# Attention layer and GAT layer: clamps, norm factors, first row and hand-over of the last graph layer

## The chip, the cores and the metric

One core of one Trainium2 chip runs the whole program. The metric is device time in microseconds (us), from a run of the program without profiling; the median of several runs is compared. A profile comes from one further execution.

## The reference

Eight batches of 2048 nodes with 256 features pass through two layers on one 2048 x 2048 adjacency matrix.

```python
# layer 0: attention, softmax per chunk of 256 columns
scores = clip(q @ k.T / 8, -10, 10)          # 4 heads of 64
scores = where(mask == 0, -10, scores)
out = sum over chunks of softmax(scores) @ v
out = layernorm(out @ Wo.T + bo + x) * gamma + beta
x = layernorm(x + out)
# layer 1: graph attention, softmax over all neighbours
Wh = x @ W                                    # 4 heads of 64
e[i,j] = leaky_relu(s_src[i] + s_dst[j], 0.2), -inf where adj == 0
h = elu(softmax(e, over j) @ Wh)
x = layernorm(x + h)
```

## The kernel before

All matrix work is in float32. The order of instructions on each engine is written out by hand, in the order of the Python code; each engine takes its own instructions in that order, and waits by semaphores where a tile is not ready.

**Layer 0** of one batch is 64 slots (two heads, one chunk of 256 columns, 512 rows each), taken in 32 *pairs*. In a pair, TensorE makes scores (L422, tile `ps`), VectorE clips and masks them (L439), ScalarE takes the exponential (L462), TensorE multiplies with the values (L473, tile `pc`), ScalarE copies the sums out (L480), VectorE takes reciprocals (L490) and GpSimd normalizes and adds up (L497, L499). Every eighth of these 32 pairs a new group of 512 rows begins; output products (L625) and products for layer 1 (L667) of the group before stand in some of the pairs.

**Layer 1** of the batch before runs along in the same pairs (`along`). It is 128 *tiles* in 8 *units* of 16: a unit is half of the target nodes (1024) and one head, a tile is 128 source nodes. `make` writes a tile `e` (128 x 1024, VectorE, L893): the larger of a row of the targets' factors and a factor `gd` of the source, times the edge mask. `use` multiplies it into the sums `pa` (TensorE, L922), two PSUM banks of four groups of 128 targets each. In even units each bank is a tile of its own, in odd units of the last batch both banks are one tile (`psA2`). After a unit, ScalarE copies `pa` to `sums` (L934), and `close`, a generator that `rest` takes forward by a step, clamps and inverts the weight sums (L950, L951), multiplies (L961 on ScalarE; in the last batch L955 on GpSimd), applies elu (L966, L967) and writes `h1` (L971).

A pair carries four tiles. In the last batch of layer 0 (`b == B - 1`), tiles of layer 1 of the batch before are carried while `s0 < SLOTS - LATE`; with LATE = 12 this ends with pair 25, and pairs 26 to 31 run without. The 24 tiles left over follow in a written list `order`, between the steps of the last group of layer 0 (`steps`, `early`) and the four steps of `factors` (`fs`): largest value (L734, L736, L738), spread of it (L742 to L756), and the row of the targets' factors. That last one transposes the factors (L761), copies them to `flat` (64 x 128: row h*16+t holds head h, target block t), and stores them in `rowD` in DRAM. `coming.start` then loads the row of unit 0 from there, broadcast over the partitions, into `srow`, and `lift` copies it to PSUM (`rowp`, L833). R, M, U in the list are `rest`, `make`, `use`.

**The last stage** is layer 1 of the last batch, with nothing beside it (`alone`). The row of each unit is lifted to PSUM, and VectorE makes its tiles from there. Each third tile is made by ScalarE from `srow` in SBUF (L862 Relu, L863 Identity) and by GpSimd (L864, times the mask), up to LEAD = 4 tiles ahead (`make_ahead`); these tiles have three buffers. A slot of this stage takes one or two steps of `close`, then two tiles. Beside it, `Closing` finishes the groups of 512 rows of both last batches: load `x1D`, add on GpSimd (L1009), `stats` (VectorE L540, L543, and the factors L548, L549 on VectorE, L550, L551 on GpSimd), and the scaled output on ScalarE (L588). `weigh` scales the weights of the next head on GpSimd (L770).

At the end, `last` takes the two banks of the last unit, one generator each, in turn: clamp (L1034), reciprocal, product, elu, statistics, output and store.

Of the kernel before, what the change touches and what calls it, by code (L numbers as in the profile page):

```python
# [8 lines left out]
F32 = mybir.dt.float32  # L9
# [5 lines left out]
ALU = mybir.AluOpType  # L15
AX = mybir.AxisListType

P = 128
# [4 lines left out]
def adj_resnorm_kernel(  # L23
# [19 lines left out]
    nc = tc.nc  # L43
    B, N, F = x.shape
    H, D = a_src.shape
    NT = N // P
# [3 lines left out]
    D1 = D + 1  # L50
    EPS = 1e-5
# [4 lines left out]
    QT = CH // P  # L56
    CLIP = 10.0 * 8.0
    FAR = 100.0
    BANKS = (8, 8)
# [14 lines left out]
    TILES = len(UNITS) * NT  # L74
    STEP = TILES // SLOTS
    LATE = 12
    WIDE = max(BANKS)
    AHEAD_E = 5
    LEAD = 4
# [54 lines left out]
    identf = consts.tile([P, P], F32, tag="identf", name="identf")  # L134
# [394 lines left out]
    class Norm:  # L529
# [5 lines left out]

        def stats(self, ks):
            sts = []
            for k in ks:
                st = small.tile([P, 6], F32, tag="st", name="st_" + self.name, bufs=4)
                nc.vector.bn_stats(st, self.src[:, k, :])  # L540
                sts.append(st)
            for k, st in zip(ks, sts):
                nc.vector.bn_aggr(self.mv[:, k, :], st)  # L543
            if ks[-1] == QT - 1:

                self.rs = small.tile([P, QT], F32, tag="rs", name="rs_" + self.name)
                self.off = small.tile([P, QT], F32, tag="off", name="off_" + self.name)
                nc.vector.tensor_scalar(self.rs, self.mv[:, :, 1], EPS, None, ALU.add)  # L548
                nc.vector.tensor_scalar(self.off, self.mv[:, :, 0], -1.0, None, ALU.mult)  # L549
                nc.gpsimd.tensor_tensor(self.rs, self.rs, nhalf, ALU.pow)  # L550
                nc.gpsimd.tensor_mul(self.off, self.off, self.rs)  # L551
# [169 lines left out]
    def factors(b, sd, waug):  # L721
# [8 lines left out]
        st = {}  # L730
# [27 lines left out]
        def rows():  # L758

            pr = banks([P, CH], "pr1")  # L760
            nc.tensor.transpose(pr[: H * NT, :P], s.rearrange("p h t -> p (h t)"), identf)  # L761
            flat = small.tile([H * NT, P], F32, tag="flat", name="flat", bufs=1)
            nc.scalar.copy(flat, pr[: H * NT, :P])
            nc.scalar.dma_start(out=rowD[b].rearrange("h (t p) -> (h t) p", p=P), in_=flat)
            nc.gpsimd.tensor_copy(waug[:, :, :, D], ed.rearrange("p h t -> p t h"))
            for h in range(H if b + 1 < B else 1):
                weigh(h)
# [7 lines left out]

        return gd, [most, spread, rows, weigh]


    class Layer1:
        def __init__(self, b, gd, waug):  # L780
            self.b, self.gd, self.waug = b, gd, waug
            self.made = self.used = 0
            self.rows, self.edge, self.e = {}, {}, {}
            self.tail = []
            self.room = ep, "e"
            self.alone = b == B - 1
            self.masks = {}
            self.begun, self.lifted = 0, {}
# [19 lines left out]

        def start(self):
            self.load_row(0)  # L810
            if self.alone:
                self.lift(0)
                self.ngd = small.tile([P, H, NT], F32, tag="ngd", name="ngd", bufs=1)
                nc.vector.tensor_scalar(self.ngd, self.gd, -1.0, None, ALU.mult)
# [88 lines left out]
        def use(self):  # L903
# [15 lines left out]
            e = self.e.pop(k)  # L919
            for i in range(BANKS[m]):  # L920
                for z in range(2):
                    nc.tensor.matmul(  # L922
                        self.pa[i // QT][z * D : (z + 1) * D, i % QT, :],
                        lhsT=e[:, i * P + z * D : i * P + (z + 1) * D],
                        rhs=self.waug[:, j, h, :],
                        start=(j == 0 and i % QT == 0),
                        stop=(j == NT - 1 and i % QT == QT - 1),
                        skip_group_check=True,
                    )
            self.used += 1  # L930
            if j == NT - 1 and not (self.b == B - 1 and n == len(UNITS) - 1):
                raw = small.tile([P, WIDE, D1], F32, tag="sums", name="sums", bufs=1)
                for i, pa in enumerate(self.pa):
                    nc.scalar.copy(raw[:, i * QT : (i + 1) * QT, :], pa)  # L934
                self.tail.append(self.close(n, raw))

# [4 lines left out]

        def close(self, u, raw):
            m, h = UNITS[u]
# [5 lines left out]
            dn = small.tile([P, n, 1], F32, tag="dn", name="dn")  # L949
            nc.vector.tensor_scalar(dn, raw[:, :, D:D1], 1e-30, None, ALU.max)  # L950
            nc.vector.reciprocal(dn, dn)  # L951
# [113 lines left out]
    class Closing:  # L1065
# [5 lines left out]
        def do(self, s, *kinds):  # L1071
            for g, step, *more in self.table.get(s, ()):
# [10 lines left out]
                elif step == "stats":  # L1083
                    self.of[g].n.stats((0, 1, 2, 3))
                elif step == "most":
# [87 lines left out]
    for b in range(B):  # L1173
# [169 lines left out]
        else:  # L1343
# [7 lines left out]
            order += [steps[5], U, M, M, R, U, M, U, steps[6], R, steps[7], M, M, U, steps[8], R]  # L1351
            order += [U, steps[9], M, R, M, M, U, U, R, fs[0], M, U, fs[1], M, U, fs[2], coming.start]
            done = sum(p is U for p in order) + 1, sum(p is M for p in order) + 1
# [72 lines left out]
```

## Time and profile before

| | us |
|---|---|
| median of 3 runs | 3578.28 (3577.15 to 3580.79) |
| profiled execution, its own time | 3576.82 |
| its span, first to last instruction | 3575.0 |
| pairs of the last batch until 3350 | from 2990 |
| tail of layer 0, up to the row's store | 3350 to 3394.2 |
| rest of layer 1 of batch 6 | 3394.2 to 3408.4 |
| last stage | 3408.4 to 3561.7 |
| end of the last two groups | 3561.7 to 3575.0 |

The first table of the page gives the busy share of each engine: PE 98%, DVE 85%, ACT 64%, POOL 40%. PE is TensorE, PEld its weight load, DVE VectorE, ACT ScalarE, POOL GpSimd, SP the engine that only issues transfers. A row of a timeline is: start, length (us), engine, line, operation, output<-inputs, shapes, how many were merged, and in brackets how long the engine was idle before and who ended that. A row of stretches gives the length and each engine's busy time (with instructions), then the granted clock of TensorE, the share of DMA and GB/s. A product of float32 appears as two records, so a tile's 16 products are 32 records, and a tile takes 0.93 us on PE.

### The profile page before, as it was taken

The numbers are of one execution on the slowest core, as the hardware profiler recorded it, in microseconds if no ns is written. First come the engines' busy times: TensorE is split into PE (matmuls) and PEld (weight loads), VectorE is DVE, ScalarE is ACT, GpSimd is POOL, SyncE is SP. The second block draws the span as 40 slices with busy tenths as digits, with TensorE's granted clock in tenths as the row PEclk, the third lists the DMA queues.
The fourth block names the chain that finished last, engine by engine and source line by source line (L and its number), as shares of the span: only waits on it lengthen the run. The fifth ranks groups of instructions, "written<-read, shape, count | busy, mean of one in ns | idle before, by whom it ended". The sixth has DMA issues, their size and how long they took to land. (4 is left out here: it accounts for less than half of the span.)

```text
span 3575.0 us, 170176 instructions
## 1 busy us (share of the span) xinstructions
PE 3500.7 (98%) x76892; PEld 2608.3 (73%) x76892; DVE 3041.6 (85%) x3655; ACT 2301.9 (64%) x4120; POOL 1422.8 (40%) x1255
## 2 busy tenths in 40 slices
PE   8999999999999999999999999999999999999877
PEld 5666677777777777776777767777677776777677
DVE  5886699987999689996999969999599986998798
ACT  5787556656666566665676656666576665766577
POOL 1555233333443334333343334334244342433377
PEclk9999999999999999999999999999999999999999
DMA  7653333443433444433444434433443343434332
GB/s 178 151 131 81 82 103 100 109 104 101 115 108 102 100 117 116 107 106 83 127 112 109 108 86 126 112 102 96 108 125 108 105 98 102 124 106 107 89 108 68
DMA packets 719848, 386.06 MB, mean 108 GB/s; under 512 B 433040, under 2 KB 679184, under 8 KB 719120
## 3 DMA queue, kind: packets, MB, share of 16 engines
q1 hardware_dynamic: 669120, 341.48, 37.0%
q10 hardware_dynamic: 50000, 33.70, 3.0%
q8 instruction: 601, 9.85, 1.1%
q14 instruction: 127, 1.04, 0.1%
HBM read 318.11 MB, written 56.89 MB: 105 GB/s over the span
## 5 line engine op out<-in xcount | busy, mean ns | idle before, releaser
L462 ACT ACTIVATE pr<-pr 128x1024 f32<-128x1024 f32 x960 | 996.7, 1054 | 438.0 <-DVE pr L439 364.3
L439 DVE SCALAR_TENSOR_TENSOR pr<-ps,slab 128x1024 f32<-128x1024 f32 x960 | 1115.6, 1204 | 100.3 <-PE ps L422 82.6
L893 DVE SCALAR_TENSOR_TENSOR e<-srow,gd,et 128x1024 f32<-128x1024 f32 x896 | 1165.5, 1334 | 5.2
L922 PEld LDWEIGHTS pa<-waug,e 128*64 128x64 f32 x32768 | 1002.6, 139 | 210.9 <-issue 173.3
L922 PE MATMUL pa<-waug,e 128*64 128x65 f32 x32768 | 1055.1, 223 | 32.3 <-DVE e L893 17.5
L473 PE MATMUL pc<-vaug,pr 128*64 128x65 f32 x30720 | 980.4, 222 | 6.3 <-DVE pr L439 6.0
L497 POOL TENSOR_TENSOR part<-raw,rd 128x512 f32<-128x512 f32 x446 | 473.6, 1062 | 1220.7 <-DVE rd L490 1216.6
L473 PEld LDWEIGHTS pc<-vaug,pr 128*64 128x64 f32 x30720 | 937.9, 138 | 21.8 <-DVE pr L439 18.9
L422 PE MATMUL ps<-qT,kT 64*64 64x512 f32 x8192 | 942.5, 596 | 4.9 <-DVE pr L439 2.5
L422 PEld LDWEIGHTS ps<-qT,kT 64*64 64x64 f32 x8192 | 287.3, 132 | 482.0 <-issue 269.4
L480 ACT COPY raw<-pc 128x520 f32<-128x520 f32 x512 | 302.7, 591 | 493.2 <-PE pc L473 490.3
L499 POOL TENSOR_TENSOR acc<-acc,part 128x512 f32<-128x512 f32 x446 | 583.8, 1309 | 35.1
L490 DVE RECIPROCAL rd<-raw 128x8 f32<-128x8 f32 x512 | 100.3, 196 | 129.8 <-ACT raw L480 122.6
L497 POOL TENSOR_TENSOR acc<-raw,rd 128x512 f32<-128x512 f32 x64 | 66.8, 1044 | 360.8 <-DVE rd L490 360.8
L667 PE MATMUL pw<-w_sb,x1T 128*64 128x264 f32 (+1 forms) x800 | 124.2, 392 | 0.2 <-DVE pr L439 0.2
L625 PE MATMUL po<-wo_sb,qT 128*64 128x256 f32 (+1 forms) x912 | 121.2, 382 | 0.0
L366 PE MATMUL pp<-xT,wk_sb 128*128 128x512 f32 x256 | 118.3, 602 | 2.9 <-DVE xT L322 1.6
L366 PE MATMUL pp<-xT,wq_sb 128*128 128x512 f32 x256 | 117.4, 599 | 0.0
L961 ACT ACTIVATE sums<-sums,dn 128x64 f32<-128x64 f32 x448 | 117.1, 334 | 0.0
L382 PE MATMUL pv<-wv_sb,xT 128*128 128x256 f32 x512 | 116.7, 381 | 0.0
L382 PEld LDWEIGHTS pv<-wv_sb,xT 128*128 128x128 f32 x512 | 96.0, 190 | 20.1 <-issue 7.2
L893 DVE SCALAR_TENSOR_TENSOR e<-rowp,gd,et 128x1024 f32<-128x1024 f32 x86 | 104.0, 1269 | 0.0
(142 smaller groups left out, 2517.5 us busy)
## 6 DMA issues: line engine op xcount, KB each, us to landing
et<-edgeD SPq DMA_DIRECT2D x896, 128.0 KB, 2.6
slab<-clipD SPq DMA_DIRECT2D x256, 256.0 KB, 3.7
srow<-rowD SPq DMA_DIRECT2D x256, 128.0 KB, 3.5
xg<-in_x_dram SPq DMA_DIRECT2D x128, 128.0 KB, 3.2
x1D<-y ACTq DMA_DIRECT2D x32, 512.0 KB, 2.9
ctxD<-acc ACTq DMA_DIRECT2D x56, 256.0 KB, 3.7
ctx<-ctxD SPq DMA_DIRECT2D x224, 64.0 KB, 2.9
xp<-in_x_dram SPq DMA_DIRECT2D x224, 64.0 KB, 2.2
```

The costliest lines, as they stand in the source:

```text
L366: nc.tensor.matmul(pps[c], lhsT=w[:, kc, c * P : (c + 1) * P], rhs=st["xT"][:, kc, :], start=(kc == 0), stop=(kc == KC - 1),)
L382: nc.tensor.matmul(pv[:, u, :], lhsT=st["xT"][:, kc, u * P : (u + 1) * P], rhs=wv_sb[:, kc, :], start=(kc == 0), stop=(kc == KC - 1),)
L422: nc.tensor.matmul(ps[z * D : (z + 1) * D, k, :], lhsT=kT[rows, hp, t * P + z * D : t * P + (z + 1) * D], rhs=qT[rows, hp, cols], start=Tr ...
L439: nc.vector.scalar_tensor_tensor(pr, ps, -CLIP, row.unsqueeze(1).to_broadcast([P, 2, CH]), op0=ALU.max, op1=ALU.min,)
L462: nc.scalar.activation(pr, pr, AF.Exp, scale=0.125)
L473: nc.tensor.matmul(pc[z * D : (z + 1) * D, k, to], lhsT=probs[s][u][:, k, i * P + z * D : i * P + (z + 1) * D], rhs=vaug[:, KT * c + u, 2 ...
L480: nc.scalar.copy(raws[s].rearrange("p k i d -> p k (i d)"), pc[:, :, : QT * D1])
L497: engine.tensor_mul(part, raw[:, :, :, :D], rd.to_broadcast([P, 2, QT, D]))
L499: engine.tensor_add(accv, accv, part)
L667: nc.tensor.matmul(pw[z, k, : F + 2 * H], lhsT=self.x1T[:, c, u * P + z.start : u * P + z.stop], rhs=w1_sb[:, c, :], start=(c == 0), stop= ...
L893: nc.vector.scalar_tensor_tensor(e, row, self.gd[:, h, j : j + 1], self.mask(k), op0=ALU.max, op1=ALU.mult,)
L922: nc.tensor.matmul(self.pa[i // QT][z * D : (z + 1) * D, i % QT, :], lhsT=e[:, i * P + z * D : i * P + (z + 1) * D], rhs=self.waug[:, j, h ...
```

## The change

It has five parts.

1. `LATE` goes from 12 to 8: pairs 26 and 27 carry tiles of layer 1 of batch 6 as well, and 16 tiles instead of 24 are left for the list.
2. The row of unit 0 of the last stage is made by TensorE: eight products with a broadcast column of the identity matrix put eight rows of `flat` on all partitions, straight into the PSUM tile. ScalarE's tiles of unit 0 read that tile too. The load of this row and its lift are left out.
3. `stats` of the closing groups puts the two small operations L548 and L549 on GpSimd.
4. `close` in the last stage clamps from `pa` in PSUM, one instruction per bank, and no longer from `sums`.
5. Of the last four tiles, TensorE takes the products of the first bank as each tile comes; those of the second bank follow for all four together.

```diff
-    LATE = 12
+    LATE = 8
...
-        def stats(self, ks):
+        def stats(self, ks, beside=False):
...
-                nc.vector.tensor_scalar(self.rs, self.mv[:, :, 1], EPS, None, ALU.add)
-                nc.vector.tensor_scalar(self.off, self.mv[:, :, 0], -1.0, None, ALU.mult)
+                engine = nc.gpsimd if beside else nc.vector
+                engine.tensor_scalar(self.rs, self.mv[:, :, 1], EPS, None, ALU.add)
+                engine.tensor_scalar(self.off, self.mv[:, :, 0], -1.0, None, ALU.mult)
                 nc.gpsimd.tensor_tensor(self.rs, self.rs, nhalf, ALU.pow)
                 nc.gpsimd.tensor_mul(self.off, self.off, self.rs)
...
+            st["flat"] = flat
...
+        def first_row(dst):
+
+            for t in range(WIDE):
+                nc.tensor.matmul(
+                    dst[:, t * P : (t + 1) * P],
+                    lhsT=identf[: H * NT, t : t + 1].to_broadcast([H * NT, P]),
+                    rhs=st["flat"],
+                    start=True,
+                    stop=True,
+                )
...
-        def start(self):
-            self.load_row(0)
-            if self.alone:
-                self.lift(0)
+        def start(self, first_row=None):
+            if not self.alone:
+                self.load_row(0)
+            else:
+                self.lifted[0] = psA.tile([P, WIDE * P], F32, tag="psA0", name="rowp")
+                first_row(self.lifted[0])
+                self.rows[0] = self.lifted[0]
                 self.ngd = small.tile([P, H, NT], F32, tag="ngd", name="ngd", bufs=1)
                 nc.vector.tensor_scalar(self.ngd, self.gd, -1.0, None, ALU.mult)
...
+            if self.alone and k >= TILES - LEAD:
+
+                products(e, j, range(QT))
+                self.held.append((e, j))
+                if k == TILES - 1:
+                    for each in self.held:
+                        products(*each, range(QT, BANKS[m]))
+            else:
+                products(e, j, range(BANKS[m]))
...
-            nc.vector.tensor_scalar(dn, raw[:, :, D:D1], 1e-30, None, ALU.max)
+            if self.alone:
+                for i, pa in enumerate(pas):
+                    k = slice(i * QT, (i + 1) * QT)
+                    nc.vector.tensor_scalar(dn[:, k, :], pa[:, :, D:D1], 1e-30, None, ALU.max)
+            else:
+                nc.vector.tensor_scalar(dn, raw[:, :, D:D1], 1e-30, None, ALU.max)
...
-                    self.of[g].n.stats((0, 1, 2, 3))
+                    self.of[g].n.stats((0, 1, 2, 3), True)
...
-            order += [U, steps[9], M, R, M, M, U, U, R, fs[0], M, U, fs[1], M, U, fs[2], coming.start]
+            order += [U, steps[9], M, R, M, M, U, U, R, fs[0], M, U, fs[1], M, U, fs[2], lambda: coming.start(fs[4])]
```

More of the change, by code (lines that the diff above doesn't have):

```diff
@@ L774, in weigh @@
             )
-        return gd, [most, spread, rows, weigh]
+        def first_row(dst):
[7 more added lines that the diff above has]
+                )
+        return gd, [most, spread, rows, weigh, first_row]
     class Layer1:
@@ L783, in __init__ @@
             self.rows, self.edge, self.e = {}, {}, {}
-            self.tail = []
+            self.tail, self.held = [], []
             self.room = ep, "e"
@@ L919, in use, with products @@
             e = self.e.pop(k)
[L920 to L929, printed above, removed]
+            def products(e, j, tiles):
+                for i in tiles:
+                    for z in range(2):
+                        nc.tensor.matmul(
+                            self.pa[i // QT][z * D : (z + 1) * D, i % QT, :],
+                            lhsT=e[:, i * P + z * D : i * P + (z + 1) * D],
+                            rhs=self.waug[:, j, h, :],
+                            start=(j == 0 and i % QT == 0),
+                            stop=(j == NT - 1 and i % QT == QT - 1),
+                            skip_group_check=True,
+                        )
+            if self.alone and k >= TILES - LEAD:
[6 more added lines that the diff above has]
+                products(e, j, range(BANKS[m]))
             self.used += 1
@@ L934, in use @@
                     nc.scalar.copy(raw[:, i * QT : (i + 1) * QT, :], pa)
-                self.tail.append(self.close(n, raw))
+                self.tail.append(self.close(n, raw, self.pa))
         def rest(self, steps):
@@ L940, in rest, with close @@
                     self.tail.pop(0)
-        def close(self, u, raw):
+        def close(self, u, raw, pas):
             m, h = UNITS[u]
```

## The prediction

> **What bounds the kernel.** I read the page first: TensorE is busy for 98% of the span, yet its busy digits fall from 9 to 7 and 8 in the last slices. So I cut the end into stretches by engine. The last stage runs from 3408.4 to 3561.7 us; its units end where the sums are copied (L934). Columns: length, then busy time of PE, PEld, DVE, ACT, POOL.
>
> ```profile
> 3296.46:3307.10 10.64, 9.43 (x181) 6.00 (x177) 6.58 (x8) 8.81 (x16) 4.06 (x4) 1.00 0.40 97
> 3212.69:3225.63 12.94, 12.94 (x306) 9.65 (x305) 10.76 (x13) 5.86 (x9) 5.87 (x6) 1.00 0.23 64
> ...
> 3430.40:3453.90 23.50, 17.85 (x534) 17.18 (x530) 23.40 (x34) 18.14 (x24) 21.06 (x14) 0.93 0.30 90
> 3473.70:3491.60 17.90, 15.88 (x534) 15.60 (x530) 14.99 (x15) 17.61 (x23) 12.69 (x9) 1.00 0.38 120
> sum 153.50, PE 128.27 PEld 124.99 DVE 138.63 ACT 127.65 POOL 122.84; mean PE 16.03 PEld 15.62 DVE 17.33 ACT 15.96 POOL 15.35
> ```
>
> Pairs that carry tiles of layer 1 are full on PE (12.94 of 12.94); those without are not. In the last stage no engine stands out: DVE has 138.6 of 153.5 us, ACT 127.7, POOL 122.8. The second unit (3430.4) is DVE's, with POOL close behind; the fourth is ACT's.
>
> Next, DVE's timeline there, and POOL's beside it:
>
> ```profile
> 3432.56 1.79 DVE L548 TENSOR_SCALAR rs_c<-mv_c 128x4 f32<-128x4 f32 x1
> 3434.27 2.05 DVE L549 TENSOR_SCALAR off_c<-mv_c 128x4 f32<-128x4 f32 x1
> 3436.24 2.05 DVE L950 TENSOR_SCALAR dn<-sums 128x8 f32<-128x8 f32 x1
> ...
> 3434.28 3.97 POOL L864 TENSOR_TENSOR e<-e,et 128x1024 f32<-128x1024 f32 x2
> 3439.46 1.93 POOL L770 TENSOR_TENSOR waug<-waug,ed 128x1024 f32<-128x1024 f32 x1
> ```
>
> Operations on 4 or 8 elements take 1.8 to 2.05 us: they end when a POOL product ends (2.0 us). With POOL idle the same lines take 0.16. Last, the hand-over from layer 1 of batch 6 to that of batch 7:
>
> ```profile
> 3394.25 0.46 ACTq L764 DMA_DIRECT2D rowD<-flat  x1
> 3402.38 1.02 ACT L833 COPY rowp<-srow 128x1024 f32<-128x1024 f32 x1 [8.16 <-DMA srow<-rowD]
> 3407.63 0.84 ACT L934 COPY sums<-pa 128x260 f32<-128x260 f32 x2 [4.23 <-PE pa L922]
> 3408.37 1.15 ACT L862 ACTIVATE e<-srow,ngd 128x1024 f32<-128x1024 f32 x1
> ```
>
> ACT and POOL stand idle for 12 us while DVE alone makes the eight tiles left over.
>
> **The parts.**
>
> *LATE 12 to 8.* Pairs 26 and 27 now carry four tiles each. Both have an output product, as 3212.69 has: 12.94 − 10.63 = 2.31 us each, **+4.6**. PE is full there, so nothing else in them counts. In the tail, 16 tiles are left; the 14 makes and uses written between the steps stay, and eight makes after the factors (3395.55 to 3406.77) are gone, with eight of the ten uses. Unit 6 of batch 6 now ends in pair 27, so its closing moves one place up in the written order. That frees ACT of L934 before the group's finish (3379.68: the transposes come 1.2 us earlier), but its last step, L971 on DVE, now stands ahead of the maximum (L734) and waits for ACT's Relu: estimate 3390.7 instead of 3389.87. L736 needed PE anyway until 3390.93, so up to the flat row (ACT ends it at 3394.22) I count **0**.
>
> *First row.* Removed: four row DMAs on SP, the lift on ACT. The write of rowD stays, for the next rows. PE waits for the flat row, then does 8 products, 16 records. Nearest row: L382, 256 columns at 0.216 us a record; 128 columns give 0.108, so 1.7 us (0.213 each, as cold transposes took, would give 3.4). Then two uses, 2 × 0.93, and 0.3 until ACT's first Relu, as before (3408.05 to 3408.37): 3394.3 + 1.7 + 1.9 + 0.3 = 3398.2 against 3408.37, **−10.2**.
>
> PE's wait for the flat row (ACT, 3393.98 to 3394.22) holds back only these two uses; on SP the next row's load now is the first to wait for rowD's landing (some 3397), and behind it stand x1D loads that POOL's add needs four slots later: no cost.
>
> That holds only if DVE and ACT can both read the row. ACT's Relu used srow in SBUF; for unit 0 it now reads the PSUM tile that DVE reads. The row that bears on this: the mask tile, which DVE reads and then ACT.
>
> ```profile
> 40.50 0.81 DVE L272 TENSOR_SCALAR clip<-pm 128x640 int8<-128x640 bf16 x1
> ...
> 41.34 0.69 ACT L274 CAST edge<-pm 128x640 fp8e4<-128x640 bf16 x1 [0.56 <-DVE clip L272]
> ```
>
> In all 48 such pairs ACT started after DVE's end. The Trainium skill (PSUM — Partial Sum Buffer, "PSUM bank collisions raise a hardware error") says why software must order even two reads: two engines in one bank at once is an error. Free reads give −10.2. Ordered reads chain Relu and products in program order: Relu(2), e0, Relu(5), e1, clamp and reciprocal, e3, Relu(8), e4, e6, Relu(11), e7, e9; with 1.15 per Relu, 1.2 to 1.25 per tile, 0.05 per hand-over, then ACT's Identity, exp, Relu (1.25) and lift, Relu(14) begins 14.8 us after Relu(2), against 12.9 before (3408.37 to 3421.31). So 1.9 is lost: **−8.3**. I take this. Behind the new wait stand all of DVE's tiles and, with them, PE: the first starts at 3399.5, after Relu(2), which itself stands behind the copies L934, and not at 3396.1, when the row is there.
>
> *Factors on POOL.* L548 and L549, six each in the stage, held DVE for 10.7 us. POOL gets 12 operations of a kind the trace lacks. Nearest row: L551, 4 elements, 0.20 (L550, a power, 1.0, and the strided copy L765, 1.0, are the upper end). Against the change speaks the skill's GPSIMD Engine Reference, "Elementwise — side-by-side cycle accounting": GpSimd takes 1.96 times DVE's time, 0.31 here by DVE's 0.16. By the row, unit 1's two groups cost POOL 0.8, by the rule 1.25. I take the row. The new pair waits for DVE's aggregates, as the power did before, so nothing behind it on POOL waits longer than these 0.4 us a group.
>
> *Clamps from PSUM.* Seven of L950 took 7.5; now 14 like L1034 (0.16), 2.2. L1034 ran with POOL idle, but DVE's tiles from the PSUM row take 1.27 whether POOL is busy or not, whereas those from srow reach 2.9. Stretched like L950 (1.07 mean) they would cost 15. I take 0.16. They still come behind L934 by the ordering above.
>
> DVE is thus 10.7 + 5.3 = 16.0 us lighter. **What reaches the end** I read unit by unit. Unit 1: DVE's stall of some 7 us (3432.6 to 3438.3, and L548 at 3442.5) goes, and PE's gaps of 2.2 and 1.6 us with it; late next is POOL, busy without a pause from 3423.8 to 3449.7. Its tile 26 was ready at 3444.35, tile 29 at 3447.7; with the added operations 3444.8 and 3448.5. PE then ends the unit at 3451.3 instead of 3453.8; a slower clock after the new gap could cost 1. I take **−2.0**. Unit 2: PE waits for POOL and for its own issue (2.5 at 3462.59), 0. Unit 3: ACT, 17.6 of 17.9, 0. Unit 4: PE nearly full, 0. Unit 5 and the start of 6: the chain goes through POOL's h (L1009) and e, then ACT, busy until 3545, **0**. Unit 7:
>
> ```profile
> 3544.34 0.70 ACT sums L934 x2
> 3545.06 1.56 DVE dn L950
> 3546.64 0.20 DVE dn L951
> 3546.85 1.16 DVE e L893
> ...
> 3549.24 12.38 PE pa L922 x416
> 3561.72 0.17 DVE dn L1034
> ```
>
> The clamp shrinks from 1.56 to 0.32: **−1.2**, PE being nearly full from there.
>
> *Bank by bank.* The first bank would be done 1.9 instead of 0.5 us before PE's end. But unit 7's two banks are one tile, and before, the first clamp (3561.72) already waited for the very last product, although its bank was finished at 3561.1; unit 1's copies did too. So **0**; were it tracked by bank, −1.2. The held tiles block no buffer, as none is made after them; tile 127 now must be ready 2.3 us before PE's end, which it is (3559.3, less 1.2).
>
> **Sum**: 4.6 − 8.3 − 2.0 − 1.2 = −6.9. The profiled execution took 3576.8 around a span of 3575.0, so 3569.9; the median of the runs is 1.5 above it: 3578.3 − 6.9 = **3571.4 us**.
>
> **Rivals.** (B) DVE was the bound of the whole stage, and its relief passes on. For it: 138.6 of 153.5, the highest. Against: units 3, 5, 6. With half of the 16 us reaching the end instead of 3.2, the sum is −11.7: 3566.6. Free reads (−1.9) or banks tracked singly (−1.2) point the same way. (C) POOL takes back what DVE gives: unit 1 gains 0, the end 0: 4.6 − 8.3 = −3.7, 3574.6. For it: POOL's unbroken stretch. (D) Slower: POOL's new scalar operations cost like L550. At p each, if all 12 lie on POOL's chain, the sum is −6.9 + 12 (p − 0.2); it turns at p = 0.78, and at 1.4 us gives +7.5: 3585.8. Against: L551, and that units 3, 4 and 7 have slack on POOL. (E) The moved tiles merely exchange places: unlikely, since 2.31 a pair is measured, and 12 us of idle ACT are too.
>
> **Numbers.** Main case 0.42, its own range 3568.5 to 3574; B 0.32; C 0.14; D and unknown stalls 0.12. Range: below 3564.5 lies a part of B, above 3578.5 most of D, together 0.2. 0.2%, about what a measurement of this kernel can tell from no change, is 7.2 us, just beyond the main case's sum. Faster: half of the main case and B, 0.53; same: the other half, C and a little of D, 0.36; slower 0.11.
>
> **What would show it.** Periods of 12.9 in pairs 26 and 27; L862 first near 3398 + 4.6, with no lift ahead of it; in unit 0 Relu and DVE's tiles never overlapping; small POOL operations near 0.2; no L548 over 0.2 us in the stage; a second unit near 21 us, POOL full; the first L1034 still behind PE's last product. It would be wrong if POOL's new rows are long, if PE's slow clock spreads over unit 0, where it is now fed more thinly, or if the freed DVE lets units 2 to 6 shrink.

## The result and the profile after

The changed kernel takes 3572.81 us (median of 22 runs, 3569.59 to 3578.09), the kernel before, on the same chip, 3579.23 us (22 runs, 3577.15 to 3583.48). The ratio is 0.9983, 95% interval 0.9977 to 0.9990: a gain of 6.4 us. A repeat beside other kernels gave 0.9989 (0.9982 to 0.9995). The prediction had 3571.4 us, with a range of 3564.5 to 3578.5, and the time lies in it; the gain stays just under the 0.2% that the prediction set as its mark, the case that it called "same" and gave 0.36, against 0.53 for "faster". The profiled execution took 3571.87 us around a span of 3570.0.

The stretches of the changed kernel come first, in the columns of the stretches of before. Line numbers have moved: L548, L549 are now L549, L550; L588 is L589; L862 to L864 are L878 to L880; L893 is L909; L922 is L940; L934 is L962; L950 is L981; L971 is L1004; L1009 is L1042; L1034 is L1067.

```profile
3298.62:3311.60 12.98, 12.98 (x308) 9.95 (x304) 12.38 (x13) 8.94 (x16) 4.65 (x4) 1.00 0.41 113
...
3426.39:3452.21 25.82, 17.77 (x536) 17.22 (x532) 18.27 (x32) 18.14 (x24) 23.15 (x19) 0.93 0.30 91
...
3470.91:3488.84 17.93, 16.07 (x536) 15.65 (x532) 15.01 (x16) 17.65 (x24) 14.86 (x13) 1.00 0.36 118
...
sum 152.52, PE 128.12 PEld 125.36 DVE 125.41 ACT 127.63 POOL 125.04; mean PE 16.01 PEld 15.67 DVE 15.68 ACT 15.95 POOL 15.63
```

Pair 26 is full on PE, as forecast, and the fourth unit is ScalarE's and unchanged. DVE is lighter by 13.2 us over the stage (138.6 to 125.4), and yet the second unit, where this was to help, grew from 23.50 to 25.82 us. POOL is busy for 23.15 of them.

The hand-over to the last stage, from the timelines of TensorE, ScalarE and VectorE:

```profile
3399.65 2.05 PE L781 MATMUL rowp<-flat,identf 64*128 64x128 f32 x16 [0.36 <-ACT flat L765]
...
3403.30 0.84 ACT L962 COPY sums<-pa 128x260 f32<-128x260 f32 x2 [3.70 <-PE pa L940]
3404.03 1.12 ACT L878 ACTIVATE e<-rowp,ngd 128x1024 f32<-128x1024 f32 x1
...
3405.19 1.28 DVE L909 SCALAR_TENSOR_TENSOR e<-rowp,gd,et 128x1024 f32<-128x1024 f32 x1 [4.78 <-ACT e L878]
3407.66 1.28 DVE L909 SCALAR_TENSOR_TENSOR e<-rowp,gd,et 128x1024 f32<-128x1024 f32 x1 [1.18 <-ACT e L878]
```

The row's products took 2.05 us from the first start to the last end, and the first Relu starts 4.43 us behind the end of the copy to `flat`, instead of 14.15. VectorE's first tile waits for the end of ScalarE's Relu, and its second for the end of the next: two reads of one PSUM tile, one after the other. The groups of the last stage show the other small operations (busy time, mean in ns, idle time before them):

```profile
L909 DVE SCALAR_TENSOR_TENSOR e<-rowp,gd,et 128x1024 f32<-128x1024 f32 x86 | 104.2, 1270 | 8.8 <-ACT e L878 8.8
...
L981 DVE TENSOR_SCALAR dn<-pa 128x4 f32<-128x4 f32 x14 | 1.6, 152 | 6.0 <-ACT sums L962 5.9
L549 POOL TENSOR_SCALAR rs_c<-mv_c 128x4 f32<-128x4 f32 x6 | 1.4, 234 | 0.5
L550 POOL TENSOR_SCALAR off_c<-mv_c 128x4 f32<-128x4 f32 x6 | 1.4, 228 | 0.5
```

Clamps from PSUM take 0.15 us with POOL busy beside them; the factors take 0.23 each on GpSimd. VectorE waits 8.8 us for ScalarE's reads of the first row. And the second unit, from the timelines of GpSimd, ScalarE, VectorE and TensorE:

```profile
3420.93 2.02 POOL L880 TENSOR_TENSOR e<-e,et 128x1024 f32<-128x1024 f32 x1 [2.24 <-issue]
...
3442.26 0.23 POOL L549 TENSOR_SCALAR rs_c<-mv_c 128x4 f32<-128x4 f32 x1
...
3443.89 0.20 POOL L552 TENSOR_TENSOR off_c<-off_c,rs_c 128x4 f32<-128x4 f32 x1
3444.04 3.98 POOL L880 TENSOR_TENSOR e<-e,et 128x1024 f32<-128x1024 f32 x2
...
3444.12 2.08 ACT L589 ACTIVATE kT<-h,off_c,rs_c 128x256 f32<-128x256 f32 x4 [0.36 <-POOL off_c L552]
...
3446.23 2.34 DVE L1004 SCALAR_TENSOR_TENSOR h<-ee,sums 128x512 f32<-128x512 f32 x1 [7.52 <-ACT kT L589]
...
3449.82 7.82 PE L940 MATMUL pa<-waug,e 128*64 128x65 f32 x250 [2.14 <-DVE e L909]
```

Read it upwards: TensorE waits for VectorE's tile, which stands behind the write of `h` of unit 0 (L1004). This write waits 7.52 us for ScalarE's output of the second closing group (L589), which must have read these rows of the tile `h` before they are written again. The write itself then takes 2.34 us and ends 0.55 us behind GpSimd's two products beside it (3448.57 against 3448.02). ScalarE's output waits for GpSimd's factors of the group, and they stand in a queue that is busy without a pause from 3420.93 to 3448.02.

Last, the end, from the chain of work that ended last:

```profile
3540.38 0.64 ACT sums L962 x2
3541.05 0.17 DVE dn L981
3541.24 0.20 DVE dn L984
3541.45 6.35 DVE e L909 x6
...
3549.15 4.78 DVE e L909 x4
3553.98 2.58 PE pa L940 x80
3556.65 0.17 DVE dn L1067
```

The clamp of 1.56 us is now 0.17. Behind VectorE's last tile (3553.93) TensorE still has 80 records: 16 of the last tile's first bank and the 64 held ones. The last clamps begin behind the very last product.

### The profile page after: what moved, and what is told of

Its sections match the earlier page's. It is cut to its first block, busy times and chain, and to the rows that moved or that the text cites. A ratio compares the mean times of both kernels' runs of the same rounds, so it can differ in the third digit from the quotient of the medians.

```text
span 3570.0 us, 170208 instructions
## 1 busy us (share of the span) xinstructions
PE 3500.0 (98%) x76908; PEld 2606.1 (73%) x76908; DVE 3026.1 (85%) x3650; ACT 2302.1 (64%) x4119; POOL 1426.6 (40%) x1267
## 5 line engine op out<-in xcount | busy, mean ns | idle before, releaser
L909 DVE SCALAR_TENSOR_TENSOR e<-srow,gd,et 128x1024 f32<-128x1024 f32 x896 | 1165.3, 1334 | 5.1
L940 PEld LDWEIGHTS pa<-waug,e 128*64 128x64 f32 x32768 | 1001.2, 138 | 206.9 <-issue 173.1
L940 PE MATMUL pa<-waug,e 128*64 128x65 f32 x32768 | 1053.1, 223 | 27.9 <-POOL e L880 15.5
L382 PE MATMUL pv<-wv_sb,xT 128*128 128x256 f32 x512 | 116.6, 381 | 0.0
L909 DVE SCALAR_TENSOR_TENSOR e<-rowp,gd,et 128x1024 f32<-128x1024 f32 x86 | 104.2, 1270 | 8.8 <-ACT e L878 8.8
L382 PEld LDWEIGHTS pv<-wv_sb,xT 128*128 128x128 f32 x512 | 95.9, 190 | 20.3 <-issue 6.9
```

Of the source, the lines that this page charges most:

```text
L382: nc.tensor.matmul(pv[:, u, :], lhsT=st["xT"][:, kc, u * P : (u + 1) * P], rhs=wv_sb[:, kc, :], start=(kc == 0), stop=(kc == KC - 1),)
L909: nc.vector.scalar_tensor_tensor(e, row, self.gd[:, h, j : j + 1], self.mask(k), op0=ALU.max, op1=ALU.mult,)
L940: nc.tensor.matmul(self.pa[i // QT][z * D : (z + 1) * D, i % QT, :], lhsT=e[:, i * P + z * D : i * P + (z + 1) * D], rhs=self.waug[:, j, h ...
```

## The experiments

Each kernel computes the whole result. "Flat" is the end of ScalarE's copy to `flat`; a unit's length runs between ScalarE's copies of the sums (L962), unit 7's to TensorE's last product. Times are in us, from one trace each. The ratio is to the kernel before in the same set of runs, with the 95% interval.

| kernel | first Relu behind flat | unit 0 ends behind flat | unit 1 | unit 2 | unit 7 | median | ratio |
|---|---|---|---|---|---|---|---|
| before | 14.15 | 36.17 | 23.50 | 19.79 | 17.26 | 3579.23 | |
| changed | 4.43 | 26.79 | 25.82 | 18.70 | 16.15 | 3572.81 | 0.9983 (0.9977-0.9990) |
| e_again | 4.44 | 26.79 | 27.07 | 18.69 | 16.15 | 3576.09 | 0.9989 (0.9982-0.9995) |
| e_before_late8 | 8.82 | 31.28 | 23.08 | 19.49 | 17.26 | 3579.20 | 0.9996 (0.9987-1.0004) |
| e_late12 | 14.15 | 36.50 | 25.82 | 18.71 | 16.15 | 3580.45 | 1.0002 (0.9994-1.0010) |
| e_own_copy | 4.44 | 25.34 | 26.49 | 20.25 | 16.15 | 3576.28 | 0.9989 (0.9980-0.9997) |
| e_dve_factors | 4.43 | 26.78 | 25.82 | 18.26 | 16.15 | 3575.24 | 0.9987 (0.9980-0.9993) |
| e_clamp_sums | 4.43 | 26.78 | 25.84 | 18.71 | 17.59 | 3579.72 | 0.9997 (0.9989-1.0006) |
| e_no_bank | 4.44 | 26.79 | 25.81 | 18.69 | 15.81 | 3576.32 | 0.9986 (0.9978-0.9994) |
| e_early_closing | 4.44 | 26.79 | 22.04 | 18.69 | 16.15 | 3571.56 | 0.9974 (0.9964-0.9984) |
| e_before_early | 14.15 | 35.60 | 21.89 | 18.26 | 17.26 | 3576.96 | 0.9992 (0.9984-1.0000) |
| e_early_dve | 4.43 | 26.79 | 21.29 | 18.25 | 16.15 | 3567.35 | 0.9968 (0.9957-0.9979) |
| e_own_early | 4.43 | 25.31 | 23.85 | 18.72 | 16.15 | 3570.42 | 0.9973 (0.9964-0.9982) |
| e_own_early_dve | 4.43 | 25.31 | 21.21 | 18.25 | 16.14 | 3569.06 | 0.9969 (0.9957-0.9981) |

Medians are compared through the ratios: the kernel before had 3579.90 beside e_own_copy, e_dve_factors, e_clamp_sums and e_no_bank, 3579.83 beside e_again, e_early_closing, e_own_early and e_before_late8, 3580.00 beside e_before_early, e_early_dve and e_late12, and 3580.34 beside e_own_early_dve.

### The changed kernel again

> The changed kernel once more, beside the others of this job. Theory: pairs 26 and 27 12.9 us each, first Relu 4.4 us behind the flat row, unit 1 at 25.8 us. The stretch from pair 30 to the flat row (55.1 us in the profile of the changed kernel, 56.4 to 56.7 in three of its variants) and unit 4 (14.5) should vary by 1 to 1.6 us between executions if they belong to TensorE's clock and not to an edit; the rival, that they belong to the kernel, expects 55.1 and 14.5 again.

No edit. Where no clock is in play, the structure repeats to 0.02 us: the first Relu, units 2, 3 and 7, and TensorE's last wait in unit 1, which ends 50.22 us behind flat in the one trace and 50.20 in the other. Other parts do not repeat: pair 30 to flat took 55.07 us in the first trace and 56.73 here, unit 1 25.82 and 27.07 (at granted clocks of 0.93 and 0.81), unit 5 19.34 and 20.93. Unit 5 in the stretches of the first trace:

```profile
3503.30:3522.64 19.34, 15.83 (x536) 15.55 (x532) 18.93 (x33) 16.22 (x17) 17.48 (x13) 1.00 0.18 58
```

and of the repeat:

```profile
3506.68:3527.61 20.93, 17.42 (x535) 17.14 (x531) 18.97 (x32) 16.23 (x17) 18.70 (x13) 0.92 0.18 54
```

The same products keep PE busy for 1.59 us more at a granted clock of 0.92, and the unit is longer by just that. The Trainium skill (TensorE: Matmul & The Clock Gate, "What's actually happening") says that the clock follows a free-running window, so that it depends on the run where a ramp falls; these two traces agree in that the same code met it in one execution and not in the other. Tail, unit 1 and unit 5 together are 4.5 us in this pair of traces (1.66 + 1.25 + 1.59), so one trace of each kernel can't carry a sum of 5 us, and units are compared below with their clocks. Unit 4 took 14.46 and 14.83, at a clock of 1.00 in both, a smaller difference than the 1 to 1.6 us expected of the clock; it ranges from 14.44 to 16.86 over the variants of the changed kernel and from 15.81 to 16.05 over the three of the kernel before. The longer ones go with a wait of TensorE late in the unit, up to 1.2 us, that the profile gives to its own issue; what moves it stays open.

### LATE alone, and all but LATE

> The kernel before with four tiles in pairs 26 and 27 and no other edit: the first row still comes through the row DMAs and ACT's lift. Theory: pairs 26 and 27 at 12.9 us, +4.6; the first Relu falls from 14.15 to about 10.3 us behind the flat row, since the DMA that was hidden behind eight tiles is now waited for (the lift began 8.2 us behind the flat row's DMA issue), -3.9; sum +0.7, so about 3580, and of the 9.7 us that the row gains in the changed kernel some 6 need TensorE's row. Rival: the row DMA is hidden anyway, the first Relu comes at 4.4 to 6 us, and the time falls by 3 us or more.

```diff
 # in the kernel before
-    LATE = 12
+    LATE = 8
```

ScalarE's timeline of e_before_late8:

```profile
3398.91 0.24 ACT L763 COPY flat<-pr 64x128 f32<-64x128 f32 x1
...
3406.49 1.02 ACT L833 COPY rowp<-srow 128x1024 f32<-128x1024 f32 x1 [7.33 <-DMA srow<-rowD]
3407.44 0.65 ACT L934 COPY sums<-pa 128x260 f32<-128x260 f32 x2
3407.97 1.16 ACT L862 ACTIVATE e<-srow,ngd 128x1024 f32<-128x1024 f32 x1
```

The transfer that eight tiles had hidden is now waited for: lift, copies and Relu follow each other without a gap. The first Relu gains 5.3 us (14.15 to 8.82; 3.9 was expected), the pairs cost 4.6 (12.94 each), and the time is 0.9996: about nothing, as the theory said. TensorE's row is needed for the other 4.4 us (8.82 to 4.43).

> The changed kernel with twelve slots without tiles, as before the change, and everything else kept. Theory: pairs 26 and 27 fall to 10.6 us each, -4.6; the eight tiles stand again between the factors and unit 1, and the start of ACT's Relu is set by DVE's eight makes behind the factors and no longer by the row: about 10 us later. Sum +5 against the changed kernel, near 3579, and TensorE's row is worth nothing there. Rival: the eight tiles need not come first, and unit 0's end moves by less than 3 us: the time falls by 2 us against the changed kernel.

```diff
 # in the changed kernel
-    LATE = 8
+    LATE = 12
```

ScalarE's and VectorE's timelines of e_late12:

```profile
3395.36 0.24 ACT L765 COPY flat<-pr 64x128 f32<-64x128 f32 x1
...
3409.01 0.84 ACT L962 COPY sums<-pa 128x260 f32<-128x260 f32 x2 [13.41 <-PE pa L940]
...
3396.93 11.29 DVE L909 SCALAR_TENSOR_TENSOR e<-srow,gd,et 128x1024 f32<-128x1024 f32 x8
```

The eight tiles stand in front again, and the first Relu is back at 14.15, to the hundredth that of the kernel before, though the row is there early. The ratio is 1.0002. So neither LATE alone nor the four other parts without it gain, and together they gain: LATE opens a hole that only TensorE's row fills.

### The first row copied for ScalarE

> The changed kernel, but ScalarE copies the first row from PSUM into SBUF as soon as TensorE has made it (1.0 us, while ScalarE would wait for TensorE anyway), and makes its tiles of unit 0 from that copy. Theory A, ordered reads of one PSUM tile cost 1.6 us: VectorE's first tile starts 2.4 us earlier, Relu of tile 14 comes 13.0 instead of 14.5 us after that of tile 2, and the kernel gains 1.5 us on the changed one. Rival: the ordering is hidden behind GpSimd's queue in the second unit: less than 0.5 us.

```diff
 # in the changed kernel
-                self.rows[0] = self.lifted[0]
+                self.rows[0] = small.tile([P, WIDE * P], F32, tag="srow", name="srow")
+                nc.scalar.copy(self.rows[0], self.lifted[0])
```

VectorE's, then TensorE's timeline of e_own_copy (the added line moves later line numbers by one):

```profile
3404.70 2.48 DVE L910 SCALAR_TENSOR_TENSOR e<-rowp,gd,et 128x1024 f32<-128x1024 f32 x2 [2.37 <-ACT srow L829]
...
3407.41 4.81 DVE L910 SCALAR_TENSOR_TENSOR e<-rowp,gd,et 128x1024 f32<-128x1024 f32 x4
...
3450.22 9.40 PE L941 MATMUL pa<-waug,e 128*64 128x65 f32 x250 [2.56 <-DVE e L910]
```

With ScalarE reading its own copy, VectorE makes four tiles in one go, and the fifth Relu starts 12.94 us behind the first instead of 14.49: the cost of the ordered reads is 1.55 us, shown by taking it away. Unit 0 ends 1.45 us earlier, and GpSimd's queue passes this on: TensorE's last wait in unit 1 ends 48.71 us behind flat (3450.22 - 3401.51), instead of 50.22. What is lost after that, this trace loses at a lower clock. The last 70 records of unit 1 then take 3.1 us instead of 2.4, and unit 2 ran at 0.87 in this trace, where the changed kernel had 1.00, and took 20.25 instead of 18.70. The ratio, 0.9989, can't show 1.5 us with an interval of some 3 us to either side, so whether the clock takes it in most executions stays open.

### The factors back on VectorE

> The changed kernel with the factors of the closing groups made on VectorE again. Theory A (the last stage is paced by hand-overs between GpSimd, ScalarE and TensorE; VectorE's time matters at few places): -1 to +2.5 us against the changed kernel, although VectorE gets some 10 us of stalled operations back; the second unit stays at 24 to 26 us because its write of h1 still waits for the second closing group's output. Theory B (VectorE was the bound, and its relief passes on): +5 us or more, the second and sixth unit each longer by some 3 us.

```diff
 # in the changed kernel
-                    self.of[g].n.stats((0, 1, 2, 3), True)
+                    self.of[g].n.stats((0, 1, 2, 3))
```

Unit 1 stays at 25.82 us. VectorE is stretched again (its L549, L550 take 1.80 and 2.04 us there), its write of `h` waits 1.69 instead of 7.52, and the tile that TensorE waits for comes 1.3 us sooner behind flat (48.9 against 50.2). This doesn't arrive, since the products behind that wait ran at half the clock. The stretch of e_dve_factors from TensorE's wait to the end of unit 1:

```profile
3449.30:3453.01 3.71, 3.69 (x72) 3.69 (x74) 3.54 (x3) 0.00 (x0) 0.87 (x1) 0.54 0.81 241
```

In the changed kernel the corresponding 72 records took 2.35 us at a clock of 1.00. Unit 2 is 0.44 shorter, at a clock of 1.00 in both, and this holds through the table: at that clock unit 2 takes 18.25 to 18.26 us in the four kernels with the factors on VectorE and 18.69 to 18.72 in the seven with them on GpSimd. Unit 5, at a clock of 0.92, takes 20.48 where the repeat took 20.93, since TensorE waits 2.29 instead of 2.74 us for GpSimd's tile. The ratio, 0.9987, lies between the two of the changed kernel: theory A's bounds hold, and moving the factors to GpSimd brought nothing that can be measured.

### The clamps back on the copied sums

> The changed kernel with the clamps reading sums in SBUF again. Theory A: +1.2 us against the changed kernel, all of it in the last unit (16.2 becomes 17.3 us), where the clamp of the unit before stands ahead of the tiles; elsewhere stalls of 1.5 to 2 us come back on VectorE without effect. Theory B: +3 to +5 us.

```diff
 # in the changed kernel
-            if self.alone:
-                for i, pa in enumerate(pas):
-                    k = slice(i * QT, (i + 1) * QT)
-                    nc.vector.tensor_scalar(dn[:, k, :], pa[:, :, D:D1], 1e-30, None, ALU.max)
-            else:
-                nc.vector.tensor_scalar(dn, raw[:, :, D:D1], 1e-30, None, ALU.max)
+            nc.vector.tensor_scalar(dn, raw[:, :, D:D1], 1e-30, None, ALU.max)
```

VectorE's timeline of e_clamp_sums at the start of the last unit:

```profile
3548.23 1.60 DVE L978 TENSOR_SCALAR dn<-sums 128x8 f32<-128x8 f32 x1 [4.12 <-ACT sums L962]
```

One clamp of 1.60 us, on the chain of unit 7, lengthens this unit by 1.44 (16.15 to 17.59); unit 1 does not notice (25.84). Over the stage, eight clamps take 7.2 us where fourteen from PSUM take 1.6. The Trainium skill (SBUF — State Buffer, "SBUF: two separate sides") describes a port pair of VectorE and GpSimd that one holds for a whole instruction; the clamps agree with it: in SBUF they took 0.90 us in the mean and up to 1.93, from PSUM 0.15 and at most 0.16. The time rose more than unit 7 explains: 0.9997 against 0.9983 and 0.9989, and 3.4 to 4.5 us over the medians of the three other variants in the same set of runs, which is what theory B had expected. Units 4 and 5 of its trace are longer too (16.86, 20.93). For unit 5 the repeat above shows the same length without the edit; in unit 4 TensorE has two waits on its own issue (0.75 and 1.18 us), which nothing ties to the clamps. So 1.44 us are shown to be the clamp's, and whether the other 2 to 3 us are stays open.

### The last tiles in one piece

> The changed kernel without the bank-by-bank order of the last four tiles. Theory A (a wait on a PSUM tile covers the whole tile): within 0.5 us of the changed kernel, the first clamp of the end still right behind TensorE's last product. Rival (banks are waited for singly): +1.2 us.

```diff
 # in the changed kernel
-            if self.alone and k >= TILES - LEAD:
+            if False:
```

VectorE's timeline of e_no_bank:

```profile
3551.13 4.86 DVE L909 SCALAR_TENSOR_TENSOR e<-rowp,gd,et 128x1024 f32<-128x1024 f32 x4
3558.38 0.16 DVE L1067 TENSOR_SCALAR dn<-pa 128x4 f32<-128x4 f32 x1 [2.39 <-PE pa L940]
```

The last clamp waits for the last product here too, 2.39 us behind VectorE's last tile instead of 2.73 in the changed kernel, and unit 7 is 0.34 shorter. Bank by bank therefore gains nothing at the end, since both banks are one tile, and costs 0.3: VectorE's last tile sets the end, and more products are left behind it. In the medians this doesn't show: the ratio, 0.9986, lies between the two of the changed kernel.

### The closing groups two steps earlier

> The closing groups of batch 6 begin two steps earlier. Theory: unit 1 is late because DVE's write of h for unit 0 (7.5 us of waiting) stands behind ACT's output of the second closing group, which stands behind GpSimd's factors of that group. With the group two steps earlier the wait falls by 2 to 4 us and unit 1 from 25.8 to 22 to 24 us; the time is 2 to 3 us below the changed kernel. Rival: GpSimd's total work paces unit 1 and the order in it is of no account: unit 1 stays within 0.5 us of 25.8, and the time within 1 us.

```diff
 # in the changed kernel
-        0: [(0, "load", kT, 0)],
-        2: [(1, "load", kT, 1)],
-        4: [(0, "pool")],
-        6: [(1, "pool")],
-        8: [(0, "stats")],
-        9: [(2, "load", kT, 2)],
-        10: [(1, "stats")],
-        11: [(0, "finish")],
+        0: [(0, "load", kT, 0), (1, "load", kT, 1)],
+        2: [(0, "pool")],
+        4: [(1, "pool")],
+        6: [(0, "stats")],
+        8: [(1, "stats")],
+        9: [(2, "load", kT, 2), (0, "finish")],
+        11: [(1, "finish")],
         12: [(3, "load", kT, 3)],
-        13: [(1, "finish")],
```

VectorE's and TensorE's timelines of e_early_closing:

```profile
3443.56 2.52 DVE L1004 SCALAR_TENSOR_TENSOR h<-ee,sums 128x512 f32<-128x512 f32 x1 [3.56 <-ACT sums L1000]
...
3434.89 7.39 PE L940 MATMUL pa<-waug,e 128*64 128x65 f32 x192 [2.31 <-POOL e L880]
3443.62 7.29 PE L940 MATMUL pa<-waug,e 128*64 128x65 f32 x234 [1.33 <-POOL e L880]
```

The write of `h` no longer waits for L589 but for its own input, and for half as long. Unit 1 falls by 3.8 us to 22.04, at the same clock (0.92, 0.93 in the first trace of the changed kernel), and beside the repeat of the changed kernel the median falls by 4.5 us, from 3576.09 to 3571.56; 2 to 3 were expected. GpSimd does the same work, but both its adds L1042 lie in unit 0, where the changed kernel's queue had a pause of 2.24 us. So the order counts, and not the total of GpSimd's work alone. The edit takes the wait away and one add of 2.4 us out of unit 1 at once; no run moves only the write behind VectorE's next tiles, which would part the two.

> The kernel before with the closing groups of batch 6 two steps earlier and no other edit. Theory: before, DVE was stopped in unit 1 by its own stretched factor and clamp operations and not by ACT's output (its write of h waited for nothing), so the earlier group gains little there: unit 1 stays at 22.5 to 24 us (23.5 before), and the time within 1.5 us of the kernel before. Rival: the order of the closing is a gain by itself that has nothing to do with the change: unit 1 falls by 3 us or more here too, and the time by 3 us.

The same edit in the kernel before. Unit 0 ends 0.6 us earlier and unit 1 falls by 1.6 to 21.89, at clocks of 0.92 and 0.93. (Unit 2 is 1.5 shorter, but ran at 1.00 here and at 0.91 in the trace of before.) The ratio is 0.9992 (0.9984 to 1.0000). So the earlier order is worth something by itself: in unit 1 more than the theory's bound and less than the rival's 3 us, in the medians the rival's 3 us (3580.00 to 3576.96). The theory had overlooked that the factors move too: in unit 1 two of VectorE's small operations are stretched (1.80 and 1.99 us), where there were four. With the change the order is worth 3.8 us in unit 1.

> The changed kernel with the earlier closing and the factors back on DVE. Theory: with the wait for ACT's output gone, the relief of DVE that was worth nothing in unit 1 is worth something: with the factors on DVE unit 1 lasts 23 to 24.5 us instead of 22.0 (two to four operations stretched to 2 us, less GpSimd's 0.9), the time 1 to 3 us above the earlier closing alone. Rival: GpSimd's chain alone sets unit 1, which stays at 22.0 +- 0.5 or falls by the 0.9 us that GpSimd no longer spends.

```diff
 # in e_early_closing
-                    self.of[g].n.stats((0, 1, 2, 3), True)
+                    self.of[g].n.stats((0, 1, 2, 3))
```

VectorE's, then TensorE's timeline of e_early_dve:

```profile
3424.18 1.66 DVE L549 TENSOR_SCALAR rs_c<-mv_c 128x4 f32<-128x4 f32 x1
3425.76 1.96 DVE L550 TENSOR_SCALAR off_c<-mv_c 128x4 f32<-128x4 f32 x1
...
3441.05 0.82 DVE L1004 SCALAR_TENSOR_TENSOR h<-ee,sums 128x512 f32<-128x512 f32 x1 [0.42 <-ACT sums L1000]
...
3428.95 18.25 PE L940 MATMUL pa<-waug,e 128*64 128x65 f32 x564 [4.10 <-DVE e L909]
```

I had expected unit 1 to be 1 to 2.5 us longer; it is 0.75 shorter (21.29), and unit 2 0.44 shorter. VectorE has its two stretched operations again (3.6 us), TensorE waits 4.10 us for its tile at the start of the unit, and then runs to the end without one more wait: GpSimd is no longer in front of it. The clock is 0.92 in unit 1 of both kernels. By the trace the rival was right: with the order mended, GpSimd's amount of work counts. With 3567.35 us, 0.9968 (0.9957 to 0.9979), this kernel has the lowest median of all; the changed kernel had 0.9983 and 0.9989 in two other sets of runs. Against e_early_closing alone (0.9974, 0.9964 to 0.9984) the intervals overlap, so the time doesn't show the factors' part.

### The row's copy on top

> The earlier closing together with ACT's copy of the first row in SBUF. Theory: the copy alone started e0's follower 2.4 us earlier and lost this in units 1 and 2, since the write of h stands behind the closing group; with that group earlier too, the 1.5 us of unit 0 remain, and the time is 1 to 2 us below the earlier closing alone, about 3568. Rival: GpSimd's queue is full whatever the order, the 1.5 us are lost again, and the time is that of the earlier closing alone.

The edits of e_own_copy and e_early_closing together. Unit 0 gains 1.48, but unit 1 is 1.8 longer (23.85 against 22.04). The stretch from TensorE's last wait in unit 1 to its end, of e_own_early:

```profile
3443.20:3450.71 7.51, 7.44 (x200) 7.45 (x202) 7.30 (x5) 4.36 (x5) 6.14 (x4) 0.77 0.76 232
```

and of e_early_closing:

```profile
3443.60:3449.73 6.13, 6.09 (x200) 5.95 (x202) 6.13 (x5) 4.31 (x5) 5.71 (x3) 1.00 0.60 174
```

The last wait ends 41.72 us behind flat instead of 42.72, so GpSimd passes on 1.0 of the 1.48; the same 200 records then take 1.35 us more, at 0.77 instead of 1.00. The medians of the two, from one set of runs, are 1.1 us apart in favour of the copy, the ratios 0.0001. Neither theory is settled by the time; by the trace, GpSimd's queue keeps a third of the gain, and the clock took the rest in this execution.

> The earlier closing, the factors on DVE and ACT's copy of the first row together. Theory: GpSimd's queue sets the end of unit 1 as long as it is unbroken; with the factors on DVE it had 2.3 us of waiting inside unit 1, so the copy's gain in unit 0 (1.5 us, 26.8 to 25.3) now passes through and unit 1 stays within 0.6 us of the 21.3 that it had with the earlier closing and the factors on DVE: 1 to 1.5 us below that kernel, ratio to the kernel before near 0.9964. Rival: as with the factors on GpSimd, unit 1 gives back 1.5 to 1.8 us (22.8 to 23.1) and the time does not move.

The same with the factors on VectorE. Unit 0 has the 1.48 us, and unit 1 keeps its length (21.21 against 21.29) as the theory said, though with the better clock of the two (1.00, 0.92), so that the trace alone doesn't prove it. The medians (3569.06 of 6 runs, 3567.35 of 7 runs of e_early_dve; ratios 0.9969 and 0.9968, each with an interval of 0.11 to 0.12% to either side) can't show 1.5 us, so its worth in time stays open.

## Why the prediction came out as it did

The steps of the sum, with the profiled pair beside them (before against after, us), and the repeat where it differs. The ordered reads are taken up to the start of GpSimd's unbroken stretch (29.54 us behind flat before, 21.33 after), and unit 1 from there to its end:

| step | predicted | measured | repeat |
|---|---|---|---|
| pairs 26 and 27 | +4.6 | +4.65 | +4.95 |
| tail up to flat | 0 | -1.43 | +0.23 |
| first Relu behind flat | -10.2 | -9.72 | |
| ordered reads | +1.9 | +1.51 | |
| unit 1, beyond the row | -2.0 | +1.15 | +2.4 |
| unit 2 | 0 | -1.09 | |
| units 3 and 6 | 0 | -0.01 | |
| unit 4 | 0 | -1.59 | -1.22 |
| unit 5 | 0 | +0.41 | +2.00 |
| unit 7 | -1.2 | -1.11 | |
| end behind the last product | 0 | +0.04 | |
| ahead of pair 26 (same code) | | +2.16 | +1.96 |

The column of the first pair adds up to -5.03, the difference of the spans. At like clocks unit 2 is not shorter but 0.44 longer (18.26 us in e_before_early, 18.70 in the changed kernel), and the edits account for 4.65 - 9.72 + 1.51 + 1.15 + 0.44 + 0.41 - 1.11 = -2.7. Unit 4 gives some -0.9 more, if the mean of the table's kernels is taken for both sides (16.0 for three of the kernel before, 15.1 for ten of the changed one without e_clamp_sums). The medians say -6.4 and -3.7. The traces of before and after are one draw each; the start of pair 26 shows it, at 3296.5 in the trace of before and at 3296.7 to 3300.1 in the others, with the same code ahead of it in all. The tail is another such draw: 75.05 to 76.72 us over the eleven kernels with LATE 8, 76.49 in the trace of before.

**Pairs.** Right: PE is full in a pair with tiles, and 12.94 could be read off a neighbour.

**First row.** Right in mechanism and size. The products' records start 0.112 us apart, where 0.108 was taken from L382; with a first step of 0.21 and the last record's own 0.27 they took 2.05 us, not 1.7, and the Relu came 4.43 us behind flat where 4.0 was counted. The choice between free and ordered reads was right as well: 1.51 of the predicted 1.9, and the copy takes it away. The skill's reason (PSUM — Partial Sum Buffer, "PSUM bank collisions raise a hardware error") fits, but no run tests what would happen without the order.

**Unit 1.** This is the step that failed: "DVE's stall of some 7 us goes, and PE's gaps of 2.2 and 1.6 us with it; late next is POOL". The stall did go, and POOL did become late, by what had been counted: its unbroken stretch grew from 25.94 us (3423.76 to 3449.70) to 27.09 (3420.93 to 3448.02). Each operation took 0.23 us, nearer to the row of 0.20 than to the 0.31 estimated from the ratio in the skill's GPSIMD Engine Reference ("Elementwise — side-by-side cycle accounting"), which was measured with 2048 elements; yet the four cost 1.15 with the gaps between them, nearer to the 1.25 of that estimate than to the row's 0.8. But the unit did not end behind POOL's last tile, which was ready at 3446.03, 6 us ahead of the end. The write of `h` stands in VectorE's order ahead of the tiles that end the unit, and it needs the closing group's output, which needs POOL. In the kernel before, from the timelines of ScalarE, VectorE and GpSimd:

```profile
3446.38 2.06 ACT L588 ACTIVATE kT<-h,off_c,rs_c 128x256 f32<-128x256 f32 x4
...
3449.14 1.10 DVE L971 SCALAR_TENSOR_TENSOR h<-ee,sums 128x512 f32<-128x512 f32 x1
...
3445.70 4.00 POOL L864 TENSOR_TENSOR e<-e,et 128x1024 f32<-128x1024 f32 x2
```

Before, VectorE reached this write 25.4 us behind the start of POOL's stretch because it was stalled itself, 0.7 us after ScalarE's output was done (3448.44): of its 7 us of stall no more than these 0.7 could have been saved here. Now it writes at 25.3 us, because it waits there: 7 us of stall became 7.52 us of waiting. The write also ends about 0.5 us behind POOL's products in both kernels (3450.24 and 3449.70 before, 3448.57 and 3448.02 after; the same in e_dve_factors, e_early_closing and e_early_dve), so a later POOL stretches it, from 1.10 to 2.34 us, and from its end to the end of the unit there are 3.6 us in both. From the start of POOL's stretch, unit 1 thus ends after 31.28 us instead of 30.13: all of POOL's 1.15 came through, by way of the stretched write, and nothing of VectorE's relief did. (The unit's own length grew by 2.3, since unit 0, which POOL does not end, gained 1.17 more than the start of POOL's stretch.) I had looked at what VectorE's freed time would let TensorE do, and not at the next wait in VectorE's own queue. e_early_closing takes that wait away and gets 3.8 us in this unit; by the trace of e_early_dve the factors are better on VectorE even then, by 1.2 us in units 1 and 2.

**Unit 7 and the banks.** Right to 0.1 us for the unit; e_clamp_sums shows that it is the clamp. That the last clamp waits for the whole tile was right. "tile 127 now must be ready 2.3 us before PE's end, which it is" missed the point: PE ends 2.6 us behind that tile, held by it, and the held products cost 0.3 us instead of nothing.

**Units 2, 4 and 5.** All three were counted as 0. Unit 2 shrank by 1.1 in the pair of traces: the trace of before had a clock of 0.91 there (so had e_before_late8, with 19.49), that of the changed kernel 1.00, and at like clocks it grew by 0.44. Unit 5 grew by 0.4 at a clock of 1.00 in both. e_dve_factors takes both away, so they are the price of the factors on GpSimd, which the prediction had counted in unit 1 alone; the earlier closing brings the 0.4 of unit 5 as well (e_before_early, 19.35). For unit 4 the cause stays open.

**The rivals.** C, that POOL takes back what VectorE gives, describes unit 1 better than the main case, and its -3.7 is close to what the steps add up to with unit 4 (-3.6) and to the repeat's median; only its "the end 0" is wrong. B, that VectorE was the bound of the whole stage, falls for the factors, most of the relief: e_dve_factors gives them back and loses nothing that can be measured. For the clamps the traces show the 1.1 us of unit 7 and no more, while the time of e_clamp_sums leaves room for 2 to 3 us beyond it. D needed operations of 0.78 us and got 0.23. E, that the tiles merely exchange places, is what LATE does without TensorE's row: 0.9996. The prediction stood in its range because the row and the pairs, which carry the sum, were read off rows of the trace; and its -6.9 lies near the first median partly by chance, since unit 1 was missed by 3 us and nothing in the edits makes these up.

## What to carry to other kernels

When an engine is relieved of stalls, follow its own queue to the next instruction that waits, and ask when that one could start at the earliest: a stall that only covered a wait returns as this wait. Move work off the engine with the highest busy share only onto one whose queue has a pause at that place; here the order of a queue was worth 3.8 us in one unit, where moving the factors between queues was worth nothing or less. And two edits of which neither gains alone can gain together, so the parts of a change are tested both alone and left out.

## What was not expected of the hardware

- The same code met TensorE's lower clock in one execution and not in the next: unit 5 at 1.00 and at 0.92, worth 1.6 us, and in unit 1 of e_dve_factors 3.7 us at 0.54 behind a wait of 2.56 us, which cost just the 1.3 us that had been gained ahead of it.
- Small GpSimd operations on 128x4 elements took 0.23 us, 1.5 times VectorE's 0.16 with GpSimd idle, with 0.09 us between the two factors of a group, which need nothing from each other.
- VectorE's write of `h` (128x512, two inputs in SBUF) ended about 0.5 us behind the end of a GpSimd product in both kernels, whether it began 0.56 us ahead of that end (before, 1.10 us long) or 1.79 us (after, 2.34 us long).
